# A Fourier layer's mix stage: the spectrum loaded block-diagonal from DRAM, and the row transform back on a half-sample grid

## The chip, the core and the metric

The kernel runs on one core of a Trainium2 chip. The metric is device time in microseconds from start to end of one execution. The core has a matrix engine (TensorE, PE in the profile, with its weight loads as PEld), three engines for elementwise work (VectorE or DVE, ScalarE or ACT, GpSimd or POOL) and SyncE (SP), whose queue issues most DMA transfers; POOL issues the others. Data lies in DRAM, in SBUF (128 lanes, called partitions) and in PSUM, where matmuls write. Everything is in float32, and each float32 matmul appears in the trace as two passes, each with its own weight load.

## What is computed

The input `x` is 16 images of 16 channels of 256 x 256. Two layers run one after the other, each as `x + layer(group_norm(x))`. The change lies in the first, a Laplace neural operator; the second (small convolutions, an involution and a channel gate) is not touched. The first layer, cut to what matters here:

```python
alpha = fft2(x)                                     # per image and channel
A  = 1 / (omega1[:, None, None, None] - pole1)      # [row frequency o, in i, out k, p]
Bm = 1 / (omega2[:, None, None, None] - pole2)      # [column frequency x, i, k, q]
S  = einsum('ikpq,oikp,xikq->oxik', residue, A, Bm)
output_residue1 = einsum('biox,oxik->bkox', alpha, S)
x1 = ifft2(output_residue1).real
# x2: a second term from the poles, summed elsewhere
return x1 + x2 / Nx / Ny
```

For every pair of frequencies `(o, x)` a 16 x 16 complex matrix `S` mixes the channels of all images; then the spectrum is transformed back. Since the images are real, about half of the row frequencies `o` suffice.

## The kernel before

**The stages.** `layer0_forward` transforms the images and writes the spectrum to DRAM as `al[33, 2, 64, 16, 256]`: 33 groups of four row frequencies, real and imaginary part `v`, 64 = (frequency `j` or `f` of the group, channel), image `b`, column frequency `x`. `layer0_mix`, the stage that changes, forms `S`, mixes and transforms back along the columns into `hd` in DRAM. `layer0_back` transforms back along the rows and adds `x2`. `layer1` is the second layer. The stages run one after the other.

**The forward transform of columns** (`wxn`, L1436 to 1443) uses a table of cosines and sines; its even and odd column frequencies stand in the two halves of a row, so the 256 values of `al` have a parity in front and the frequency behind.

**The mix stage, group by group (L752 to 779).** The order on PE, ACT, DVE and POOL is the order in which the code is written; SP and the DMA transfers follow by their dependences. For one group `g`:

- `mix` (L669) computes, for each of the 256 column frequencies `i`, one matmul (line 679) with the weights `s[:, i]`, 128 lanes by 32 columns, and as moving operand `alb[:, i]`, 64 columns. `alb` is block-diagonal: its 128 lanes are the parts, channels and four row frequencies, its 64 columns are four blocks of 16 images, and a lane is nonzero only in the block of its own frequency. Four column frequencies run side by side in four column strips of PE. ACT copies each 16 x 64 block of results from PSUM to `y` (L686).
- `residues` (L648) makes `s` for the next group: eight calls, each with matmuls (line 656) of `lt` by the table `tt`, and a copy out of PSUM by DVE or ACT (L665, L667). `s` exists once, so it begins when the mix has ended. `lt` comes from `poles` (L634), three DVE products (L640) from the plane-wise reciprocals `av`, which `load_poles` fetches two groups ahead on SP.
- `turn` (L688) transposes `y` for one row frequency `f` on PE, and DVE and ACT copy the result to `yt`.
- `columns` (L704) transforms back along the columns: for two halves `q`, even and odd column frequencies `e`, two `c` and two parts `v` a matmul (line 714) with `yt` as weights (64 lanes by 128 columns) and 256 columns of the table `ix`. Even and odd sums stand in one PSUM tile `ph`. ACT copies the odd half to SBUF (L723); DVE forms `even + odd` and `even - odd`, the two halves of the row (L726, L727), in the tile `h`, of which there are five buffers. POOL issues two stores to `hd` for each `q` (L734). For `f` of 3 the columns are spread into the mix of the next group (`between`).
- `load_spectrum(g, q)` (L602) fetches a quarter of the group's spectrum (four images) into one of four buffers `alc`, in four transfers of 32 lanes by 4 KB each, on SP (L607). `expand` (L613) multiplies a buffer by a lane mask `m4` into one of the four column blocks of `alb` and so writes data and zeros alike: 16 expansions for a group, six on ACT (L617) and ten on DVE (L619), dealt out by `spreads` (L622) between the turns and columns of the group before. `alb` exists once, 64 KB of every lane, its innermost order being frequency block and image.

Of the kernel before, what the change touches and what calls it, by code (L numbers as in the profile page):

```python
# [10 lines left out]
F32 = mybir.dt.float32  # L11
# [554 lines left out]
def layer0_mix(ctx, tc, d, al, hd, tabs):  # L566
# [32 lines left out]
    pst = ctx.enter_context(tc.tile_pool(name="pst", bufs=2, space=PSUM))  # L599
    psh = ctx.enter_context(tc.tile_pool(name="psh", bufs=2, space=PSUM))  # L600

    def load_spectrum(g, q):  # L602

        t = gp.tile([P, 4, 2, P], F32, tag="alc", name="alc", bufs=4)
        src = al[g].rearrange("v (j h c) b x -> h (v j) c (b x)", h=4, c=4)
        for h in range(4):
            nc.sync.dma_start(  # L607
                out=t[32 * h : 32 * h + 32].rearrange("p b e x -> p (b e x)"),
                in_=src[h, :, :, 4 * q * N : 4 * q * N + 4 * N],
            )  # L610
        return t

    def expand(t, q, j, eng):  # L613

        dst = alb.rearrange("p (x e) j b -> p b e x j", e=2)[:, 4 * q : 4 * q + 4, :, :, j]
        if eng is nc.scalar:
            eng.activation(dst, t, AF.Copy, scale=m4[:, j : j + 1])  # L617
        else:
            eng.tensor_scalar(dst, t, m4[:, j : j + 1], None, ALU.mult)  # L619


    spreads = (  # L622
# [4 lines left out]
    )  # L627

    def spread(spectrum, f):
        for eng, parts in zip((nc.scalar, nc.vector), spreads[f]):  # L630
            for q, j in parts:
                expand(spectrum[q], q, j, eng)

    def poles(av):  # L634


        lt = lp.tile([P, 32, 3, 4, 4], F32, tag="lt", name="lt")
        shape = [P, 32, 4, 4]
        for plane in range(3):
            nc.vector.tensor_tensor(  # L640
                lt[:, :, plane],
                av[:, :, :, plane].unsqueeze(3).to_broadcast(shape),
                m16.unsqueeze(1).unsqueeze(2).to_broadcast(shape),
                ALU.mult,
            )
        return lt.rearrange("p (k g) l f c -> p k g l f c", g=4)

    def residues(lt, s, k0):  # L648

        kk = k0 // 2  # L650
        ps = psg.tile([P, 2, 2, N], F32, tag="pg", name="ps")
        for v in range(2):
            for g in range(4):
                for odd in range(2):
                    lanes = slice(64 * odd, 64 * odd + 64)
                    nc.tensor.matmul(
                        ps[32 * g : 32 * g + 32, odd, v],
                        lhsT=lt[lanes, kk, g, 1 - v : 3 - v].rearrange("p l f c -> p (l f c)"),
                        rhs=tt[lanes, kk, g],
                        start=True,  # L660
                        stop=True,
                    )
        dst, src = s[:, :, :, k0 : k0 + 2], ps.rearrange("p k v x -> p x v k")
        if kk % 2:
            nc.vector.tensor_copy(dst, src)  # L665
        else:
            nc.scalar.copy(dst, src)  # L667

    def mix(s, y, between):  # L669


        for x0 in range(0, 64, 16):
            if x0 >= 32:
                next(between, None)
            ps = psg.tile([P, 16, 64], F32, tag="pg", name="pg")
            for x in range(16):
                for q in range(4):
                    i = 4 * (x0 + x) + q
                    nc.tensor.matmul(  # L679
                        ps[32 * q : 32 * q + 32, x],  # L680
                        lhsT=s[:, i].rearrange("p v k -> p (v k)"),
                        rhs=alb[:, i].rearrange("p j b -> p (j b)"),
                        start=True,
                        stop=True,
                    )
            nc.scalar.copy(y[:, :, x0 : x0 + 16], ps.rearrange("p x j -> p j x"))  # L686
# [16 lines left out]

    def columns(g, f, yt):  # L704

        ph = [psh.tile([P, 2, N], F32, tag="ph", name="ph") for q in range(2)]
        for e in range(2):
            if e:
                yield
            for n, (c, v) in enumerate(((0, 0), (0, 1), (1, 0), (1, 1))):  # L710
                i = 2 * (2 * c + e) + v
                for q in range(2):
                    lanes = slice(64 * q, 64 * q + 64)
                    nc.tensor.matmul(  # L714
                        ph[q][:, e],
                        lhsT=yt[lanes, i].rearrange("p t k -> p (t k)"),
                        rhs=ix[lanes, i],
                        start=n == 0,
                        stop=n == 3,
                    )  # L720
        for q in range(2):
            odd = hp.tile([P, 2, P], F32, tag="odd", name="odd", bufs=2)
            nc.scalar.copy(odd, ph[q][:, 1].rearrange("p (v x) -> p v x", v=2))  # L723
            o = hp.tile([P, 2, 2, P], F32, tag="h", name="h", bufs=5)
            even = ph[q][:, 0].rearrange("p (v x) -> p v x", v=2)
            nc.vector.tensor_tensor(o[:, :, 0], even, odd, ALU.add)  # L726
            nc.vector.tensor_tensor(o[:, :, 1], even, odd, ALU.subtract)  # L727
            o = o.rearrange("p v h x -> p v (h x)")
            fy = 4 * g + f
            for v in range(2):  # L730

                if fy % P or v == 0:
                    part = fy // P if fy % P == 0 else v
                    nc.gpsimd.dma_start(  # L734
                        out=hd[fy % 2, part, fy % P // 2, q:nb:2].rearrange("b k x -> b (k x)"),
                        in_=o[:, v],
                    )

    E = mybir.EngineType
    with tc.manual_schedule(engines={E.PE, E.Activation, E.DVE, E.Pool}):  # L740
# [6 lines left out]
        for q in range(4):  # L747
            spread(spectrum, q)
        for q in range(4):
            spectrum[q] = load_spectrum(1, q)  # L750
        between = iter(())
        for g in range(NF):  # L752
            more = g + 1 < NF
            y = gp.tile([P, 64, 64], F32, tag="y", name="y")
            if more:
                lt = poles(av)
            mix(s, y, between)
            if more:
                s = gp.tile([P, N, 2, C], F32, tag="s", name="s")
                residues(lt, s, 0)  # L760
            for f in range(4 if more else 1):
                if more and f == 3:
                    spread(spectrum, f)
                    for k0 in (12, 14):
                        residues(lt, s, k0)
                yt = turn(y, f)
                if more:
                    for k0 in range(2 if f == 0 else 4 * f, 4 * f + 4, 2) if f < 3 else ():
                        residues(lt, s, k0)
                    if f < 3:  # L770
                        spread(spectrum, f)
                    if g + 2 < NF:
                        if f == 0:
                            av = load_poles(g + 2)
                        spectrum[f] = load_spectrum(g + 2, f)
# [646 lines left out]
def fourier_tables():  # L1422
# [5 lines left out]
    def parities(a):  # L1428
# [4 lines left out]
    fy[:, 0, 1, 0] = cos[:P, P]  # L1433
    wx = np.stack([cos, -sin, sin], axis=1)

    wxn = np.stack(  # L1436
        [
            np.stack([np.concatenate([cos[:P, e::2], -sin[:P, e::2]], 1),
                      np.concatenate([sin[:P, e::2], cos[:P, e::2]], 1)], axis=1)
            for e in (0, 1)  # L1440
        ],
        axis=1,
    )

    ix = np.stack([np.concatenate(a, 1) for a in ((cos[:, :P], sin[:, :P]), (-sin[:, :P], cos[:, :P]))], 1)
    ix = np.tile(ix.reshape(64, 8, N), (2, 1, 1))

    iy = np.stack([cos[:P], -sin[:P]], axis=1) / (N * N)
    iy[0, 0] *= 0.5
# [6 lines left out]
    for t in tt:  # L1456
# [21 lines left out]
        "m4": np.tile(np.repeat(np.eye(4), 4, axis=0), (8, 1)),  # L1478
# [76 lines left out]
```

## Time and profile before

| what | value |
|---|---|
| median of 3 runs | 6919.16 us (6918.71 to 6933.95) |
| the profiled execution | 6939.37 us, span 6937.6 us, mean granted clock 0.967 |
| forward, 0 to 1381 us | PE busy 1244.8 us, DVE 1094.7, DMA share 0.42 |
| mix stage, 1381 to 2781 us | PE busy 1204.2 us, DVE 869.6, ACT 802.8, POOL 439.6, DMA share 0.36 |
| back, 2781 to 3430 us | PE busy 602.3 us, DMA share 0.93 |
| second layer, 3430 to 6937 us | PE busy 3324.0 us, DVE 2928.1, DMA share 0.85 |

The rows on the stages are the busy times of the engines in stretches of the trace. In the groups of instructions of the mix stage, `L714 PE MATMUL ph` takes 507.9 us in all, the mix's `L679 PE MATMUL pg` 311.6, the residues' `L656` 272.4, the transposes' `L695` 141.6; the expansions take 424.1 us of DVE (330 of 1415 ns) and 387.5 us of ACT (198 of 2059 ns). A group line reads: line, engine, operation, written tile, read tiles, sizes, count, then busy time, mean length in ns, and idle time before it with what ended it. "issue" means that nothing in the profile explains the wait. "DMA share" is the mean busy share of the 16 DMA engines. The rows on code transfers are called "instruction".

### The profile page before, as it was taken

The numbers are of one execution on the slowest core, as the hardware profiler recorded it, in microseconds if no ns is written. First come the engines' busy times: TensorE is split into PE (matmuls) and PEld (weight loads), VectorE is DVE, ScalarE is ACT, GpSimd is POOL, SyncE is SP. The second block draws the span as 40 slices with busy tenths as digits, with TensorE's granted clock in tenths as the row PEclk, the third lists the DMA queues.
The fourth block names the chain that finished last, engine by engine and source line by source line (L and its number), as shares of the span: only waits on it lengthen the run. The fifth ranks groups of instructions, "written<-read, shape, count | busy, mean of one in ns | idle before, by whom it ended". The sixth has DMA issues, their size and how long they took to land.

```text
span 6937.6 us, 153382 instructions
## 1 busy us (share of the span) xinstructions
PE 6375.2 (92%) x59944; PEld 3583.2 (52%) x59944; DVE 5451.1 (79%) x10057; ACT 3703.9 (53%) x5732; POOL 3635.8 (52%) x4614
## 2 busy tenths in 40 slices
PE   7899989978888888899789999999999999999996
PEld 5777777766766677677533333333333333333331
DVE  8888987356666666788788888888888888888885
ACT  1223333355655555222376666666666666666671
POOL 2334544523333333666665666666766566665563
PEclk9999999989999999999899999999999999999998
DMA  3444434433333333999877898888988889988886
GB/s 95 124 123 122 122 112 119 113 123 104 111 108 111 110 104 93 318 327 326 281 209 231 272 285 261 264 274 277 286 267 261 272 267 285 287 262 262 272 272 211
DMA packets 715941, 1443.97 MB, mean 208 GB/s; under 512 B 101338, under 2 KB 523542, under 8 KB 672950
## 3 DMA queue, kind: packets, MB, share of 16 engines
q1 hardware_dynamic: 567030, 959.77, 45.0%
q0 software_dynamic: 148192, 474.40, 21.8%
q8 instruction: 478, 7.83, 0.5%
q14 instruction: 241, 1.97, 0.1%
HBM read 877.12 MB, written 556.47 MB: 207 GB/s over the span
## 4 chain that ended last, share of the span: by engine, by line
PE 65%; DVE 20%; DMA 5%; issue 5%; ACT 4%; POOL 1%; SPq 0%; DVEq 0%; ACTq 0%; POOLq 0%
PE c2ps L1201 17%; PE c L1053 14%; PE pd L1121 13%; PE pg L679 4%; PE ph L714 3%; DVE alb L619 3%; ACT wide L1101 3%; PE px L313 2%; PE pu L207 2%; PE py L876 2%; PE pr L1080 2%; PE pv L214 2%; DVE u L224 2%; PE py L877 2%; DVE st L174 1%
## 5 line engine op out<-in xcount | busy, mean ns | idle before, releaser
L1101 ACT ACTIVATE wide<-c,b 32x512 f32<-32x512 f32 x2176 | 1479.6, 680 | 311.6 <-PE c L1053 263.5
L1132 DVE TENSOR_TENSOR top<-pd,t 32x512 f32<-32x512 f32 x2176 | 1504.0, 691 | 52.6
L1053 PE MATMUL c<-z,w 102*128 102x512 f32 x2048 | 999.7, 620 | 110.7 <-ACT wide L1101 89.3
L1113 POOL COPY wide<-wide 32x1031 f32<-32x1031 f32 (+1 forms) x576 | 579.7, 1006 | 881.5 <-ACT wide L1101 854.4
L1129 DVE TENSOR_TENSOR t<-pd,r 64x512 f32<-64x512 f32 x1088 | 744.1, 684 | 345.3 <-PE pd L1121 298.2
L1121 PE MATMUL pd<-wide,dw 128*128 128x512 f32 x2048 | 988.6, 604 | 12.0 <-DVE top L1132 11.0
L734 POOL DMA_DIRECT2D hd<-h x512 | 434.8, 856 | 955.0 <-DVE h L727 937.0
L1053 PEld LDWEIGHTS c<-z,w 102*128 102x128 f32 x2048 | 371.7, 192 | 697.5 <-issue 462.5
L1201 PE MATMUL c2ps<-rows,c 128*32 128x512 f32 x6144 | 721.6, 602 | 5.6 <-DVE odd L1228 5.6
L1121 PEld LDWEIGHTS pd<-wide,dw 128*128 128x128 f32 x2048 | 380.9, 192 | 572.2 <-issue 418.5
L1114 POOL COPY wide<-wide 32x1031 f32<-32x1031 f32 (+1 forms) x576 | 576.0, 1000 | 33.5
L1072 ACT ACTIVATE bot<-c,b 128x512 f32<-128x512 f32 x544 | 344.4, 684 | 462.6 <-issue 381.4
L714 PE MATMUL ph<-ix,yt 64*128 64x256 f32 x4128 | 507.9, 394 | 17.6 <-DVE yt L701 14.7
L313 PE MATMUL px<-wxn,u 128*64 128x256 f32 x4224 | 481.5, 379 | 2.4 <-ACT o L320 2.4
L207 PE MATMUL pu<-fy,eo 128*128 128x128 f32 x2048 | 436.2, 297 | 42.0 <-DVE u L224 35.2
L714 PEld LDWEIGHTS ph<-ix,yt 64*128 64x128 f32 x4128 | 419.6, 192 | 89.9 <-ACT s L667 29.6
L679 PE MATMUL pg<-alb,s 128*32 128x64 f32 x16896 | 311.6, 237 | 154.1 <-issue 71.8
L1201 PEld LDWEIGHTS c2ps<-rows,c 128*32 128x32 f32 x6144 | 174.8, 108 | 513.5 <-issue 404.5
L889 POOL TENSOR_TENSOR x<-x,o 128x512 f32<-128x512 f32 x256 | 324.4, 1267 | 217.3 <-DVE o L888 197.5
L619 DVE TENSOR_SCALAR alb<-alc,m 128x1024 f32<-128x1024 f32 x330 | 424.1, 1415 | 0.0
L214 PE MATMUL pv<-at,eo 128*128 128x128 f32 x2048 | 423.0, 291 | 0.0
L726 DVE TENSOR_TENSOR h<-ph,odd 128x256 f32<-128x256 f32 x258 | 113.4, 440 | 389.4 <-ACT odd L723 389.4
(221 smaller groups left out, 11460.2 us busy)
## 6 DMA issues: line engine op xcount, KB each, us to landing
rows<-cf SPq DMA_DIRECT2D x128, 2176.0 KB
z<-zn SPq DMA_DIRECT2D x768, 257.8 KB
cf<-top POOLq DMA_DIRECT2D x512, 240.0 KB, 6.9
cf<-bot POOLq DMA_DIRECT2D x96, 840.0 KB, 10.8
alc<-al SPq DMA_DIRECT2D x528, 128.0 KB
zn<-zb SPq DMA_DIRECT2D x128, 516.0 KB
o<-zn SPq DMA_DIRECT2D x128, 516.0 KB
z<-in_x SPq DMA_DIRECT2D x64, 1024.0 KB
```

Source lines behind the costliest of these rows:

```text
L313: nc.tensor.matmul(ps[64 * k : 64 * k + 64, :, h], lhsT=u[:, h, part, g0 + j + k].rearrange("p f c -> p (f c)"), rhs=wxn[:, h, part], star ...
L619: eng.tensor_scalar(dst, t, m4[:, j : j + 1], None, ALU.mult)
L679: nc.tensor.matmul(ps[32 * q : 32 * q + 32, x], lhsT=s[:, i].rearrange("p v k -> p (v k)"), rhs=alb[:, i].rearrange("p j b -> p (j b)"), s ...
L714: nc.tensor.matmul(ph[q][:, e], lhsT=yt[lanes, i].rearrange("p t k -> p (t k)"), rhs=ix[lanes, i], start=n == 0, stop=n == 3,)
L1053: nc.tensor.matmul(ps[:, a], lhsT=w, rhs=z[:k, c : c + 2, 0:N], start=True, stop=True)
L1101: nc.scalar.activation(self.feat[64 - 32 * q : 96 - 32 * q, f, self.groups[g], :H], ps[q][32 * f : 32 * f + 32], AF.Mish, bias=b1[0][32 * ...
L1113: nc.gpsimd.tensor_copy(flat[0:32, f, 1:m], flat[64:96, f, 0 : m - 1])
L1114: nc.gpsimd.tensor_copy(flat[96:128, f, 0 : m - 1], flat[32:64, f, 1:m])
L1121: nc.tensor.matmul(ps, lhsT=dwt if self.tail else dw, rhs=self.feat[:, f, cs, :H], start=True, stop=True,)
L1129: nc.vector.tensor_tensor(t[64:128], ps[:64], self.r[:, cs], ALU.mult)
L1132: nc.vector.tensor_tensor(self.top[32 * f : 32 * f + 32, cs, q], ps[lanes], t[lanes], ALU.add)
L1201: nc.tensor.matmul(ps[32 * j : 32 * j + 32], lhsT=w[:, blk], rhs=src[:, 4 * j + blk : 4 * j + blk + 4, x : x + H], start=(i, blk) == (0, 0 ...
```

## The change

**The spectrum.** `alb` gets the order lane, frequency block `f`, image `b`, column frequency `x`, and is cleared once at the start, half by DVE and half by POOL. `load_spectrum(g)` writes each piece of a group's spectrum from DRAM into its own diagonal block: 16 transfers for a group, for each `f` and each quarter `h` of the channels, onto 8 lanes (two parts by four channels), 16 KB for each lane. The blocks off the diagonal stay zero. The buffers `alc`, the mask `m4`, `expand`, `spreads` and `spread` go. The transfers for group `g + 1` stand after `mix` of group `g`, since the one `alb` is read until then. In `mix` the moving operand is `spectra[:, :, x]`: its 64 columns lie 1 KB apart.

**The transform back.** The forward table `wxn` takes its frequencies at half-sample positions (`cosh`, `sinh` of `(2k + 1)k'`), and `ix` correspondingly. On that grid the four quarters of a row are sums and differences of two symmetric and two antisymmetric sums of 64 columns, so `ix` has 128 columns for 256. `columns` makes as many matmuls as before, each with 128 columns, into blocks of `ph` chosen by the part `v`. ACT copies the antisymmetric half; DVE forms their sum and, mirrored, their difference in a tile `w`; from the two parities of `w` DVE forms the outer quarters and POOL the inner ones, mirrored.

**The poles.** `lt` is laid out by part, so that `poles` is two products of 1024 elements for each lane where it was three of 512, and a weight load of `residues` reads consecutive elements.

```diff
-    ix = load(nc, cp, d["ix"], [P, 8, N], "ix")
-    alb = cp.tile([P, N, 4, nb], F32, name="alb")
-    m4 = load(nc, cp, d["m4"], [P, 4], "m4")
+    ix = load(nc, cp, d["ix"], [P, 8, P], "ix")
+    alb = cp.tile([P, 4, nb, N], F32, name="alb")
+    nc.vector.memset(alb[:, :2], 0.0)
+    nc.gpsimd.memset(alb[:, 2:], 0.0)
+    spectra = alb.rearrange("p f b x -> p (f b) x")
...
-    def load_spectrum(g, q):
-        t = gp.tile([P, 4, 2, P], F32, tag="alc", name="alc", bufs=4)
-        src = al[g].rearrange("v (j h c) b x -> h (v j) c (b x)", h=4, c=4)
-        for h in range(4):
-            nc.sync.dma_start(
-                out=t[32 * h : 32 * h + 32].rearrange("p b e x -> p (b e x)"),
-                in_=src[h, :, :, 4 * q * N : 4 * q * N + 4 * N],
-            )
-        return t
+    def load_spectrum(g):
+        src = al[g].rearrange("v (f h c) b x -> h f v c (b x)", f=4, h=4)
+        for f in range(4):
+            for h in range(4):
+                lanes = slice(32 * h + 8 * f, 32 * h + 8 * f + 8)
+                nc.sync.dma_start(
+                    out=alb[lanes, f].rearrange("p b x -> p (b x)"), in_=src[h, f]
+                )
...
-        lt = lp.tile([P, 32, 3, 4, 4], F32, tag="lt", name="lt")
-        shape = [P, 32, 4, 4]
-        for plane in range(3):
+        lt = lp.tile([P, 2, 32, 4, 2, 4], F32, tag="lt", name="lt")
+        shape = [P, 128, 2, 4]
+        for v in range(2):
             nc.vector.tensor_tensor(
-                lt[:, :, plane],
-                av[:, :, :, plane].unsqueeze(3).to_broadcast(shape),
-                m16.unsqueeze(1).unsqueeze(2).to_broadcast(shape),
+                lt[:, v].rearrange("p k f l c -> p (k f) l c"),
+                av.rearrange("p k f l -> p (k f) l")[:, :, 1 - v : 3 - v].unsqueeze(3).to_broadcast(shape),
+                m16.unsqueeze(1).unsqueeze(1).to_broadcast(shape),
                 ALU.mult,
             )
...
-                        rhs=alb[:, i].rearrange("p j b -> p (j b)"),
+                        rhs=spectra[:, :, N // 2 * (i % 2) + i // 2],
...
-            for n, (c, v) in enumerate(((0, 0), (0, 1), (1, 0), (1, 1))):
-                i = 2 * (2 * c + e) + v
-                for q in range(2):
-                    lanes = slice(64 * q, 64 * q + 64)
-                    nc.tensor.matmul(
-                        ph[q][:, e],
-                        lhsT=yt[lanes, i].rearrange("p t k -> p (t k)"),
-                        rhs=ix[lanes, i],
-                        start=n == 0,
-                        stop=n == 3,
-                    )
+            for v in range(2):
+                blocks = slice(0, 4, 3) if v == 0 else slice(1, 3)
+                for c in range(2):
+                    i = 2 * (2 * c + e) + v
+                    for q in range(2):
+                        lanes = slice(64 * q, 64 * q + 64)
+                        nc.tensor.matmul(
+                            ph[q][:, e, blocks],
+                            lhsT=yt[lanes, i].rearrange("p t k -> p (t k)"),
+                            rhs=ix[lanes, i].rearrange("p (b x) -> p b x", b=2),
+                            start=c == 0,
+                            stop=c == 1,
+                        )
...
-            odd = hp.tile([P, 2, P], F32, tag="odd", name="odd", bufs=2)
-            nc.scalar.copy(odd, ph[q][:, 1].rearrange("p (v x) -> p v x", v=2))
-            o = hp.tile([P, 2, 2, P], F32, tag="h", name="h", bufs=5)
-            even = ph[q][:, 0].rearrange("p (v x) -> p v x", v=2)
-            nc.vector.tensor_tensor(o[:, :, 0], even, odd, ALU.add)
-            nc.vector.tensor_tensor(o[:, :, 1], even, odd, ALU.subtract)
+            anti = hp.tile([P, 2, 2, 64], F32, tag="anti", name="anti", bufs=2)
+            nc.scalar.copy(anti, ph[q][:, :, 2:])
+            w = hp.tile([P, 2, 2, 2, 64], F32, tag="w", name="w")
+            sym = ph[q][:, :, :2]
+            nc.vector.tensor_tensor(w[:, 0], sym, anti, ALU.add)
+            nc.vector.tensor_tensor(w[:, 1, :, :, ::-1], sym, anti, ALU.subtract)
+            o = hp.tile([P, 2, 4, 64], F32, tag="h", name="h", bufs=5)
+            parts = o.rearrange("p v s x -> p s v x")
+            nc.vector.tensor_tensor(parts[:, 0::3], w[:, :, 0], w[:, :, 1], ALU.add)
+            nc.gpsimd.tensor_tensor(parts[:, 2:0:-1], w[:, :, 0], w[:, :, 1], ALU.subtract)
...
-        spectrum = [load_spectrum(0, q) for q in range(4)]
+        load_spectrum(0)
...
             mix(s, y, between)
             if more:
+                load_spectrum(g + 1)
                 s = gp.tile([P, N, 2, C], F32, tag="s", name="s")
                 residues(lt, s, 0)
```

More of the change, by code (lines that the diff above doesn't have):

```diff
@@ L704, in columns @@
     def columns(g, f, yt):
-        ph = [psh.tile([P, 2, N], F32, tag="ph", name="ph") for q in range(2)]
+        ph = [psh.tile([P, 2, 4, 64], F32, tag="ph", name="ph") for q in range(2)]
         for e in range(2):
@@ L769, in layer0_mix @@
                         residues(lt, s, k0)
[L770 to L775, printed above, removed]
+                    if f == 0 and g + 2 < NF:
+                        av = load_poles(g + 2)
                 between = columns(g, f, yt)
@@ L1434, in fourier_tables @@
     wx = np.stack([cos, -sin, sin], axis=1)
+    half = np.outer(2 * k + 1, k) % (2 * N) * (TWO_PI / (2 * N))
+    cosh, sinh = np.cos(half), np.sin(half)
     wxn = np.stack(
         [
-            np.stack([np.concatenate([cos[:P, e::2], -sin[:P, e::2]], 1),
-                      np.concatenate([sin[:P, e::2], cos[:P, e::2]], 1)], axis=1)
+            np.stack([np.concatenate([cosh[:P, e::2], -sinh[:P, e::2]], 1),
+                      np.concatenate([sinh[:P, e::2], cosh[:P, e::2]], 1)], axis=1)
             for e in (0, 1)
```

29 lines of the change are left out of this document (6 added, 23 removed), and 4 rows, old and new, of the table spreads.

## The prediction

> **What bounds the kernel now.** I read the page first, then the mix alone: its busy time by engine, its waits, the timeline of one group, and the DMA rows of four stretches. In the timeline (start us, length us, engine, line, operation, count, idle before) one group, from the mix at 2003.88 to the next at 2045.67, is:
>
> ```profile
> 2003.88 3.45 PE L679 MATMUL pg<-alb,s 128*32 128x64 f32 x160 [2.08 <-DVE s L665]
> 2009.21 2.79 PE L679 MATMUL pg<-alb,s 128*32 128x64 f32 x96 [1.88 <-issue]
> ...
> 2011.93 2.00 PE L714 MATMUL ph<-ix,yt 64*128 64x256 f32 x16
> ...
> 2017.70 1.99 PE L679 MATMUL pg<-alb,s 128*32 128x64 f32 x128
> ...
> 2023.08 3.72 PE L714 MATMUL ph<-ix,yt 64*128 64x256 f32 x32
> ...
> 2028.28 19.01 SPq L607 DMA_DIRECT2D alc<-al  x16
> ...
> 2045.67 3.32 PE L679 MATMUL pg<-alb,s 128*32 128x64 f32 x125 [2.16 <-DVE s L665]
> ```
>
> The first mix starts at 1412.55 and the 33rd at 2754.86, so a group lasts 1342.3/32 = 41.95 us. PE is busy 87% of it and sets the pace. Two parts: the mix itself, 2003.88 to 2019.7 (in the next group 2045.67 to 2061.8, so 16.2 us), though its passes need only 4 x 1.99 us and the two half columns 2 x 2.0; and 25.7 us of residues, turns and columns, closed by a wait of 2.16 us for DVE's copy of `s`, which stands behind the expansions. The 4 us missing in the mix are "issue": code comes in pieces of 16 KB, and the DMA rows of 2003 to 2020 show
>
> ```profile
> q8 instruction: 4, 0.07, 1.6%
> ```
>
> four pieces for 576 passes, one per 3.6 us or so. The spectrum costs nothing today: four `alc` buffers are refilled behind the expansions, long before they are wanted.
>
> **The part that decides: the load.** The expansions and the masks go. The spectrum is written straight into `alb`, of which there is one copy (64 KB of each lane), and every matmul of the mix reads all lanes of it. So group g+1's 16 transfers start when the last `pg` pass of group g has ended, and mix g+1 starts when the last of them has landed. The period becomes mix + load, and all other work lies inside the load. How fast is the load? It moves the same 2.097 MB, but a transfer is now `[v=2, c=4, 4096]` from DRAM onto 8 lanes, where it was `[(v j)=8, c=4, 1024]` onto 32. How many of the 16 DMA engines take part is seen in two stretches in which only one kind of hardware transfer runs. First `alc`, with a backlog behind it (windows, last columns clock, DMA share, GB/s; then its DMA rows):
>
> ```profile
> 1389.00:1395.00 6.00, 4.16 (x96) 2.15 (x96) 1.73 (x2) 2.11 (x2) 0.00 (x0) 0.58 1.00 413
> 1396.00:1403.00 7.00, 2.84 (x96) 1.49 (x80) 4.76 (x5) 4.30 (x4) 0.00 (x0) 0.85 0.51 200
> ```
>
> ```profile
> DMA packets 427, 1.40 MB, mean 200 GB/s; under 512 B 85, under 2 KB 85, under 8 KB 427
> ```
>
> 85 of 427 packets are tiny and 342 hold 4 KB: 8 tiny ones to each transfer's 32. The share is 0.51 although transfers are queued (issue began at 1389): the same 8 engines each time. Its outer source dimension is 8, its destination has 32 lanes. Next the 24 loads of ten rows onto ten lanes at L1044 (3560 to 3580):
>
> ```profile
> q1 hardware_dynamic: 486, 1.00, 17.9%
> ...
> z<-zn SPq DMA_DIRECT2D x24, 40.2 KB
> ```
>
> 486/24 = 20: 10 rows and 10 tiny packets, where 16 engines would give 26 and a count of 624. So a transfer runs on as many engines as its smaller outer dimension counts. In the new load that is v = 2. I take 2 engines, always the same ones, as with `alc`; the other end, 8 engines by its lanes, is rival A.
>
> [...]
>
> Each of two engines then moves 1.049 MB. Per busy engine the windows give 413/16 = 25.8 GB/s, where larger packets run, and 200/(0.51 x 16) = 24.5 for 4 KB ones; with the `hd` stores in between, 1500 to 2700 gives q1 64.77 MB in 16.8% of 16 x 1200 us, or 20.1. The packets will be 16 KB, so I take 25.8: 40.6 us (ends 38, from 437 GB/s in the fullest slices of that stretch, and 52). The `hd` stores use all 16 engines,
>
> ```profile
> q0 software_dynamic: 36242, 59.53, 17.5%
> ```
>
> which is 0.175 x 41.95 = 7.3 us of each engine per group by packet time, 5.1 by bytes; three of four columns fall into the load: 4 us (0 to 5.5). Issue to first use: the chain of waits has 2.94 us from an `alc` issue's end to the expansion, of which 16 KB per engine are 0.67; with the 0.65 of one issue, 3.0 us (2.5 to 3.5); the other 15 issues (273 to 650 ns each) are hidden by the stream. Load: 40.6 + 4 + 3 = 47.6 us.
>
> On SP only `load_poles(g+2)` stands behind the waiting loads. It reaches the same two engines after them, so DVE's `poles` of the next group start when the mix does; the `lt` they write is wanted after the mix, 16 us later.
>
> **The mix.** Same passes, same code bytes, 16.2 us. Shorter column halves inside it give code no more speed, so I count no gain; the pause before it lets perhaps 2 us of code wait ready, and its low clock takes something back (14 to 18). The moving operand now has its 64 elements 1 KB apart. No row shows a strided one on PE. DVE's strided write at L224 takes 588 ns against 440 for the same size packed: from 1.0 to 1.34, and 1.34 x 1.99 = 2.7 us per 128 passes still lies under the 3.6 of code. I take nothing. [...]
>
> **What is hidden.** Per group: ACT loses 6 x 2.06 = 12.4 us, DVE 10 x 1.415 = 14.2. DVE gains 8 more sums of 128x256 between SBUF tiles (0.42, L546): 3.4; `poles` in two instructions of 1024 (1.24, L1191) for three of 512 (0.69): +0.4. POOL gains 8 subtractions (753 ns, L265), 6.0, ahead of the `hd` issues it already makes (16 x 0.86 = 13.8). PE: columns of 128 for 256, so 32 passes take between 1.86 us (half) and 3.35 (the weight loads' busy time) instead of 3.72. After the mix PE then has 25.7 - 2.2 - 3 x (0.4 to 1.9), or 18 to 22 us, inside 47.6. Were the cover gone, this work would be the path again, and the late `hd` stores (0.75 us of POOL each) would wait for one of five `h` buffers. The two clears of 8192 elements (3548 ns for 4128 at L1011, so 7 us) are paid once, under the first load.
>
> **The sum.** Period 16.2 + 47.6 = 63.8 us, 21.85 more, x 32 = 699. At the start the engines are full until 1395 (`tt` and `ix`; half an `ix` is 1.3 us), then 40.6 + about 2 until the first mix at 1436.5 instead of 1412.55: 24. Together +723. The profiled execution is 6939.4 us (span 6937.6 and 1.8 around it): 7662; the median shown is 20 lower, so 7642. I say 7640.
>
> **Rivals.** A: the 8 lanes decide, 8 engines. 2.097 MB at 200 GB/s is 10.5 us, with 3.0 and some `hd` under 18, within PE's 18 to 22 us. Period 34 to 38.6, 3.4 to 8 less, x 32: 6690 to 6830, say 6760, faster. For it: destination lanes are the outermost thing written; against it: `alc` had 32 lanes and used 8. It decides from 7 engines up, where the load (2.1 MB/(7 x 25.8) = 11.6, and 3 + 4) comes under PE's work. B: v and c are dealt out so that 4 engines work: 20.3 + 7 + 16.2 = 43.5, x 32 and the start: about 6975. Nothing in the rows shows such a deal. C: 8 engines, but the strided operand takes the place of the code. From 5 us per 128 passes (2.5 times the 1.99) it eats A's gain; at 4 times, 8 us, the mix is 34 us, the period 54, the time 7305. Against it: PE takes an element only about every 0.9 ns today (256 columns, 232 ns a pair).
>
> **How the numbers follow.** Two engines 0.85; A 0.09; B 0.03; C 0.03. Inside the forecast the ends are 14 + 2.5 + 38 + 0 = 54.5 (7345) and 18 + 3.5 + 42.8 + 5.5 = 69.8 (7840), or 71 with 20.1 GB/s (7880). All at one end at once is unlikely, so 7390 to 7870 holds most of the 0.85. About 0.3% can be told from no change: faster 0.10 (A and a little of B), same 0.02, slower 0.88.
>
> **What would show it.** In the mix's windows the DMA share during the load is about 0.13 for the loads alone, near 50 GB/s; before each mix PE waits some 25 us for a DMA onto `alb`; the clock sags there. DVE, ACT and POOL are idle over half of it. The `ph` passes and their length tell of the halved columns, the `pg` rows of the stride. It is wrong if the share during the load is near 0.5 and PE waits for no DMA.

## The result and the profile after

The changed kernel takes 8103.8 us (median of four runs, 8098.6 to 8114.0), the kernel before 6920.4 (median of four): a ratio of 1.1707 (95% interval 1.1687 to 1.1727). Slower, as forecast, but by 1180 us and not by 720: 8104 lies above the range of 7390 to 7870.

From the page of the changed kernel (the profile's summary of one execution): the span, the granted clock and the DMA share in 40 slices, three groups, and the DMA issues of the load.

```profile
span 8112.3 us, 152964 instructions
...
PEclk9999999878878788787899899999999999999998
DMA  3444444111111111111599878888888888888886
...
L659 PE MATMUL pg<-alb,s 128*32 128x64 f32 x16896 | 902.9, 405 | 957.0 <-DMA alb<-al 604.1
...
L708 DVE TENSOR_TENSOR w<-ph,anti 128x256 f32<-128x256 f32 x258 | 182.8, 709 | 1642.2 <-ACT anti L705 1642.2
...
L713 POOL TENSOR_TENSOR h<-w 128x256 f32<-128x256 f32 x258 | 238.4, 924 | 1730.2 <-DVE w L709 1727.9
...
alb<-al SPq DMA_DIRECT2D x528, 128.0 KB
```

In the twelve slices of the mix stage (the eighth to the nineteenth) the 16 DMA engines are busy a tenth of the time, and PE waits for a transfer onto `alb` before its `pg` passes: the load decides, as forecast. (604.1 of the 957.0 us are put down to that transfer; another 352.9 to the pole load that follows it on the same queue.) But the passes themselves have grown too. They are as many as before and as large, and their busy time went from 311.6 us (237 ns each) to 902.9 (405). Ahead of DVE's additions and POOL's subtractions these engines idle over 1600 us each.

One group in the timeline of the changed kernel (start us, length us, engine, line, operation, count, idle before):

```profile
2001.27 14.68 SPq L610 DMA_DIRECT2D alb<-al  x6
...
2038.20 13.99 PE L659 MATMUL pg<-alb,s 128*32 128x64 f32 x256 [28.45 <-DMA alb<-al]
...
2052.11 1.16 PE L696 MATMUL ph<-ix,yt 64*128 64x128 f32 x16
...
2053.21 7.57 PE L659 MATMUL pg<-alb,s 128*32 128x64 f32 x128
...
2061.80 7.65 PE L659 MATMUL pg<-alb,s 128*32 128x64 f32 x128
2061.95 7.34 ACT L705 COPY anti<-ph 128x256 f32<-128x256 f32 x2
2065.68 3.72 DVE L708 TENSOR_TENSOR w<-ph,anti 128x256 f32<-128x256 f32 x1 [48.08 <-ACT anti L705]
...
2069.48 14.38 SPq L610 DMA_DIRECT2D alb<-al  x12
...
2072.60 2.06 PE L696 MATMUL ph<-ix,yt 64*128 64x128 f32 x32
```

PE waits 28.45 us for the load, then needs 31 us for the mix; 128 `pg` passes, 1.99 us before, take 7.6. Two `anti` copies of ACT, which stand beside such passes, take 7.34 us, and 0.65 elsewhere. The half-width columns come out as forecast: 32 `ph` passes in 2.06 us (bounds 1.86 and 3.35).

The windows of the changed kernel for the load, the first half of that mix and its third quarter (busy us and count of PE, weight loads, DVE, ACT, POOL; then granted clock, DMA share, GB/s):

```profile
2020.00:2038.00 18.00, 0.00 (x0) 0.00 (x0) 0.00 (x0) 0.00 (x0) 0.00 (x0) 0.50 0.15 59
2038.00:2052.00 14.00, 13.80 (x256) 13.61 (x256) 0.00 (x0) 1.01 (x1) 0.00 (x0) 0.92 0.01 2
...
2053.00:2060.00 7.00, 7.00 (x127) 6.87 (x127) 0.00 (x0) 0.28 (x1) 0.00 (x0) 1.00 0.01 2
```

The DMA rows of the first window have for SP's queue

```profile
q1 hardware_dynamic: 88, 0.82, 10.8%
```

With the `hd` stores the DMA share is 0.15 and the rate 59 GB/s; SP's queue alone has 0.11 and, with 0.82 MB in 18 us, 46 GB/s (0.13 and 50 were forecast for the loads alone). A share of 0.108 is 1.7 of the 16 engines, so the two that were forecast. A 16 KB packet of a load took 614 ns (median of the stage), 26.7 GB/s; 64 of them on each of two engines are 39.3 us. The third line excludes the clock as the cause of slow passes: at full clock, with next to nothing else running, 127 of them fill 7 us.

From the first mix to the 33rd the period is 77.62 us (41.95 before). The stretch between mixes is 48.25, the mix 29.37 (means of 32 groups; before, 26.08 and 15.87). That makes 32 x 35.67 = 1141; the first mix starts 13 later than before, and what follows the 33rd mix's start is 20 longer, 14 of them this last mix itself. Together 1174, the difference of the two spans.

### The profile page after: what moved, and what is told of

It is laid out like the page before. It is cut to its first block, busy times and chain, and to the rows that moved or that the text cites. A ratio compares the mean times of both kernels' runs of the same rounds, so it can differ in the third digit from the quotient of the medians.

```text
span 8112.3 us, 152964 instructions
## 1 busy us (share of the span) xinstructions
PE 6722.9 (83%) x59944; PEld 3972.3 (49%) x59944; DVE 5289.3 (65%) x9953; ACT 3454.7 (43%) x5534; POOL 3742.8 (46%) x4873
## 5 line engine op out<-in xcount | busy, mean ns | idle before, releaser
L659 PE MATMUL pg<-alb,s 128*32 128x64 f32 x16896 | 902.9, 405 | 957.0 <-DMA alb<-al 604.1
L659 PEld LDWEIGHTS pg<-alb,s 128*32 128x32 f32 x16896 | 859.7, 153 | 978.1 <-issue 964.1
L708 DVE TENSOR_TENSOR w<-ph,anti 128x256 f32<-128x256 f32 x258 | 182.8, 709 | 1642.2 <-ACT anti L705 1642.2
L713 POOL TENSOR_TENSOR h<-w 128x256 f32<-128x256 f32 x258 | 238.4, 924 | 1730.2 <-DVE w L709 1727.9
L666 ACT COPY y<-pg 128x1024 f32<-128x1024 f32 x132 | 134.3, 1017 | 1661.4 <-PE pg L659 1661.4
L720 POOL DMA_DIRECT2D hd<-h x512 | 308.1, 605 | 287.7 <-DMA hd<-h 154.6
```

The lines of the kernel that those rows point to most:

```text
L659: nc.tensor.matmul(ps[32 * q : 32 * q + 32, x], lhsT=s[:, i].rearrange("p v k -> p (v k)"), rhs=spectra[:, :, N // 2 * (i % 2) + i // 2], ...
```

## The experiments

Two costs are to be told apart: the load between mixes and the operand's pitch. The rivals for the second were the pause itself (PE cold, or code late after it) and writes of the load that disturb the reads. Stretch and mix are measured in each trace as above, as means over 32 groups.

**The operand alone.** The pass takes 64 neighbouring numbers of the tile; all else stays:

```
-    rhs=spectra[:, :, N // 2 * (i % 2) + i // 2],
+    rhs=flat[:, 4096 * (i % 4) + 64 * (i // 4) : ... + 64],
```

> The changed kernel, but each matmul of the mix reads 64 neighbouring elements of `alb` (another 64 for each of the 256, spread over all four blocks), so it mixes other numbers and the output is not the reference's; the loads and their waits are as they were. Theory O (operand): 64 elements 1 KB apart feed PE several times slower than 64 neighbours. Then the mix falls from 29.3 us a group back to 14 to 16.5, the stretch between two mixes stays at 48.3, the period is some 64 us and the time 8104 - 33 x 13.5 = 7660 (7600 to 7720), which is also what the prediction's sum came to. Rival P (pause): the mix is long because PE has stood still for 28 us before it, at a low clock and with its code not fetched; then the mix stays near 29 us and the time at 8100.

Measured: 7575.3 us, ratio 1.0955 (1.0935 to 1.0975): the operand theory in its kind, 25 us below its range. The period is 61.31, and a mix ends 14.5 us after the last packet of its load, where the changed kernel needs 30.2. In this kernel a pass needs the lanes of one `f` only, so six passes of a mix go ahead while the load is under way, and the others start when it is over:

```profile
2045.98 6.48 PE L659 MATMUL pg<-alb,s 128*32 128x64 f32 x250 [10.74 <-DMA alb<-al]
```

PE has stood still for 25 us but for those six, the granted clock is 0.52 (window from 2046 to 2052), and 250 passes take 6.48 us where 256 took 13.99. So the pause is not it. Also seen in one view of both kernels, the instructions of a line (count, then ns of the shortest, the median and the longest). Of the changed kernel:

```profile
L705 ACT COPY anti<-ph x258: 372/378/5534, 1454.2 to 3944.6; 128x256 f32<-128x256 f32 x129
```

and of this one:

```profile
L705 ACT COPY anti<-ph x258: 372/374/380, 1454.3 to 3411.8; 128x256 f32<-128x256 f32 x129
```

The longest copy falls from 5534 ns to 380: PE's strided reads, not the copy's own form, had held ACT up. (It is not the load either: in the run without loads below, with the strided operand, the longest copy is 4636 ns.)

**Which pitch costs what.** One kernel gives each of eleven groups in turn another way through the tile (pitches in numbers of 4 bytes; the passes mix other numbers):

```
+    kind = (256, 1, 2, 4, 8, 16, 64, 257, "pairs", "fours", "same")[g % 11]
-    rhs=spectra[:, :, N // 2 * (i % 2) + i // 2],
+    rhs=moving(g, i),
```

> The changed kernel, with the pattern of the mix's moving operand changed from group to group (eleven patterns, three groups each): pitch 256 elements as it is, 1, 2, 4, 8, 16, 64, 257, then 32 pairs and 16 fours of neighbours 1 KB apart, and last pitch 256 with all four column strips reading the same column. It mixes other numbers; read from it is the length of the mix of each group. Theory L (lines of 16 bytes, 4 elements): pitch 1 as before (some 16 us), pitch 2 in between, pitch 4 and all above as slow as 256 (28 to 31 us), pairs as pitch 2, fours as pitch 1, and the same column no different. Theory B (banks, hit by the power of two): 257 is as fast as 1, and 64 or 256 slower than 4 or 8; pairs and fours help in proportion only. Theory S (the four strips get in each other's way): the same column is faster than 256.

The timeline of PE, one block of 128 passes each; in this order a pitch of 2, 4, 16, 64 and 257, then 256 with the same column in all strips, then 256 as in the change:

```profile
1566.05 2.38 PE L679 MATMUL pg<-alb,s 128*32 128x64 f32 x128
...
1628.69 3.98 PE L679 MATMUL pg<-alb,s 128*32 128x64 f32 x128
...
1757.74 3.96 PE L679 MATMUL pg<-alb,s 128*32 128x64 f32 x128
...
1828.80 7.77 PE L679 MATMUL pg<-alb,s 128*32 128x64 f32 x128
...
1901.81 3.97 PE L679 MATMUL pg<-alb,s 128*32 128x64 f32 x128
...
2096.75 7.77 PE L679 MATMUL pg<-alb,s 128*32 128x64 f32 x128
...
2175.28 7.08 PE L679 MATMUL pg<-alb,s 128*32 128x64 f32 x128
```

Two steps are to be seen (the whole kernel took 7777 us in its one run). At a pitch of 4, 8, 16 and 257 numbers (16 bytes and more) a block takes 4.0 us. At 64 and 256 the blocks shown take 7.1 to 7.8, nearly twice that again; over all groups they vary more, from 5.6 to 7.7 us in the changed kernel, 6.84 in the mean (902.9 us for 132 blocks). Runs of two or four neighbours within a long pitch keep PE busy 2.6 to 2.8 and 2.2 to 2.3 us in the last two blocks of a mix, the packed operand 2.0 to 2.3. None of the theories holds as written: L had a pitch of 4 as slow as 256, B had 257 as fast as 1. And that the four strips' different columns were the cost (S) is excluded: one column for all is no faster (7.77 us and 7.08). The first step lies between two numbers from each 16 bytes, 2.38 us, and one, 3.98. What makes it, and what makes 64 and 256 slower than 16 and 257, these runs do not show.

**257 in place of 256.** A column's run in `alb` gets one unused number behind it, which cuts the loads into pieces of 1 KB:

```
-    alb = cp.tile([P, 4, nb, N], F32, name="alb")
+    alb = cp.tile([P, 4, nb, N + 1], F32, name="alb")
```

> The changed kernel with one unused element behind every 256 of `alb`, so that the mix's 64 elements lie 1028 bytes apart and not 1024; the loads go on as before, in pieces of 1 KB. Computes the reference. From the sweep: pitch 257 takes 3.7 us for 128 passes where pitch 256 takes 7.4 and neighbours 2.2. Theory B+L (a doubling for a new 16-byte line at each element, a second one for the power of two): the mix falls from 29.3 to 4 x 3.7 + 2.3 = 17 us. The load grows with its packets, 1024 of 1 KB on each of two engines at 46 ns, 47 us for 39, so the stretch between is 56 for 48; period 73 for 77.6, time 8104 - 32 x 4.6 - 12 = 7945 (7850 to 8000). Rival (the sweep's gain came from what else was odd there, such as the strips' columns): the mix stays at 29 and the time goes to 8360.

Measured: 7934.7 us, ratio 1.1474 (1.1451 to 1.1496), as expected. (The 3.7 us that the expectation takes from the sweep is 4.0 in its trace, so the mix comes out at 17.8 and not at 17.) The mix falls to 17.8 us in all groups but the first, which has no columns in it (15.6), and the stretch rises to 54.3: of the 11.6 us that the better pitch gains, the smaller pieces give back 6.0. (A 1 KB packet on SP's queue takes 46 ns, the median in the trace of before, so 16 of them 736 ns; one of 16 KB takes 614 in the changed kernel.)

**No loads.** The 32 loads after the first are left out, with the operand as in the change and then packed:

```
             if more:
-                load_spectrum(g + 1)
```

> The changed kernel with the spectrum loaded once, before the first group; the other 32 loads are left out, so all groups mix with the first group's spectrum and the output is not the reference's. The load theory (the stretch between mixes is load alone, and the rest of PE's work would take 18 to 22 us there): mix 29.3, stretch 18 to 22, period 47.3 to 51.3 instead of 77.6, so 7130 to 7260 us, say 7190. Rival, that the load's writes into SBUF also slow the strided mix: they end before it begins, so the mix should not change; if it falls below 25 us, part of the mix's 29.3 belongs to the load and not to the operand. Rival, that the columns and the residues have grown too (as where the change's transform was put into the kernel before, with 28.9 us between mixes): period about 58, 7480.

> The same with the operand of a pass as 64 neighbouring numbers of the tile: other numbers of the spectrum are mixed and 32 loads are left out, the output is not the reference's. If load and stride are all that the change lost by, mix 13 to 16.2, stretch 18 to 22, period 31 to 38.2 instead of 77.6 and 41.95 before: 6610 to 6840, say 6720, faster than before. If the transform's part takes as long as it did alone in the kernel before (28.9 between mixes), the period is about 43 and the time about 7000, slower than before even then.

Measured: 7240.1 us, ratio 1.0457 (1.0423 to 1.0491), and 6729.4, ratio 0.9719 (0.9687 to 0.9751). The stretches are 20.7 and 21.1 us, inside the 18 to 22 that the prediction gave PE's remaining work; the mixes 29.5 and, after the first, 13.8. Both times lie in their ranges, and the mix has its 29 us without any load beside it. The four kernels make a square:

| | loads | no loads |
|---|---|---|
| strided | 8104 | 7240 |
| packed | 7575 | 6729 |

The stride costs 529 us with loads and 511 without, the load 864 and 846: they add up, and nothing of size lies between them. The timeline of the kernel without both, one mix:

```profile
2022.14 2.76 PE L659 MATMUL pg<-alb,s 128*32 128x64 f32 x180 [1.23 <-DVE s L645]
2026.28 1.31 PE L659 MATMUL pg<-alb,s 128*32 128x64 f32 x76 [1.38 <-issue]
```

There the wait for a transfer is gone and the unexplained wait ("issue") is back, as in the kernel before; that it is a wait for code is the prediction's reading, which no run here tests.

**More engines for the load.** `al` is laid out so that a transfer's source is eight whole rows; its lanes stay the same:

```
-    src = al[g].rearrange("v (f h c) b x -> h f v c (b x)", f=4, h=4)
+    src = al[g].rearrange("(f h c) v b x -> h f (c v) (b x)", f=4, h=4)
```

> The changed kernel with the spectrum stored as [33, 64, 2, 16, 256], so that a load's source is 8 rows of 16 KB one behind the other, onto the same 8 lanes (parts and channels change places within them, and `lt` with them). Computes the reference. Theory E (engines): the old load ran on 2 engines because its source had an outer dimension of 2; now 8 work, the load takes 10.5 + 3 + some hd, below PE's work after the mix; the stretch between two mixes falls from 48.3 to 18 to 22 us and the time to 8104 - 32 x 28 = 7200 (7100 to 7350). DMA share during the load near 0.5. Rival D (destination): 8 lanes take no more than two engines' worth, or 16 KB packets are slow by themselves; then the stretch stays over 40 us and the time near 8100.

Measured: 7767.3 us, ratio 1.1236 (1.1215 to 1.1257); the stretch is 38.2 us, not 20, and neither theory's numbers came. A window of the load in this kernel with the DMA row of SP's queue, then waits over the whole stage:

```profile
2012.00:2020.00 8.00, 6.50 (x88) 4.71 (x88) 2.87 (x7) 1.76 (x4) 2.71 (x4) 0.55 0.51 76
```

```profile
q1 hardware_dynamic: 60, 0.48, 38.9%
```

```profile
POOL hd L720 <- DMA hd<-h: 512.2, 136, 8.2
DVE h L712 <- DMA hd<-h: 492.7, 88, 12.7
...
PE pg L659 <- DVE s L645: 283.8, 30, 16.6
```

SP's queue alone now has a share of 0.39, six engines' worth, where it had 0.11. Of its 60 packets 29 are of 16 KB and 31 are tiny, so about eight tiny ones to a transfer's eight rows: counted as the prediction counted `alc`, eight engines. So far more than two take part, and the reading that the source's outer dimension held them to two was right here. But the packets are slower: a 16 KB packet takes 1851 ns (median of the stage) where two engines needed 614. From its first packet to its last the load takes 34.4 us, or 61 GB/s, for 46.0 us and 46 GB/s in the changed kernel (means of 32 groups). And it is not what PE waits for last: it is through 2.9 us before the mix begins, and PE waits 30 times, once a group, for DVE's copy of `s`. DVE waits for a free buffer `h`, whose stores take 18.2 us to land (median; 17.3 in the changed kernel, 4.2 before). Whether the eight lanes or the new order of the rows in DRAM slow the packets, this run does not show; the next ones bear on it.

**The loads on POOL's queue.** They leave SP, first alone and then with the pitch of 257:

```
-    nc.sync.dma_start(
+    nc.gpsimd.dma_start(
```

> [...] Computes the reference. Theory E2 (the same two engines every time is what makes the load slow, and the destination lanes of one transfer are what made eight engines crowd in the last attempt): if POOL's queue deals its transfers out to other engines each time, the stretch between mixes falls from 48.3 to what PE does after the mix or POOL needs for its issues, 20 to 27 us, period 49 to 56, time 8104 - 32 x 25 = 7300 (7150 to 7450). [...]

> The changed kernel with both: pitch 257 and the loads on POOL's queue. Computes the reference. If both costs are what the runs say and they add, the mix is 17 us and the stretch after it 20 to 27, a period of 37 to 44 against 41.95 of the kernel before: 6780 to 7000. Rival: the costs do not add, because a shorter mix leaves the load and the code pieces to meet; then above 7100.

Measured: 7468.6 us, ratio 1.0800 (1.0769 to 1.0830), just past the upper end, with a stretch of 29.2 us; and 7283.1, ratio 1.0531 (1.0517 to 1.0546), a mix of 17.8 and a stretch of 34.4: missed by 280 or more. In the first the load itself takes 19.1 us from its first packet to its last, 110 GB/s, with packets of 1174 ns (median). That is eight packets at a time (128 x 1174 ns in 19.1 us), about as many as with eight rows (seven). A transfer lands 7.9 us after its issue (median), so several of the 16 are under way at once, to different lanes. This speaks for the lanes as the limit there; queue and row order differ too. But the load begins 6.2 us after the mix, as POOL comes to it, and the next mix 3.9 us after the load. The waits of the second (us in total, times, longest):

```profile
PE ph L696 <- DVE yt L681: 366.3, 64, 12.5
DVE w L708 <- POOL h L713: 349.7, 54, 11.7
...
POOL alb L610 <- DMA alb<-al: 199.7, 162, 3.0
```

Read from below: POOL's issues of loads wait for earlier loads; behind them stand POOL's subtractions, behind these DVE's additions, and PE waits for DVE. A load on POOL's queue costs POOL time that PE's columns need: an issue takes 549 ns of POOL in the first, 847 in the second (medians), 16 to a group. The pitch acts here as it did alone: two `anti` copies beside the mix take 0.65 us again.

**The transform alone.** Into the kernel before go only the half-sample tables and the new `columns`; load, expansion and operand stay as before. (For a short diff see `columns`, `ix` and `wxn` of the change.)

> The kernel before with the transform back alone changed: `wxn`, `ix` and `columns` from the change, the masks and expansions kept. Computes the reference. Theory V (DVE): after the mix DVE is busy 23 of 26 us, and gets 8 sums of 0.42 more, so the shorter columns (2.06 us for 3.72, three of them in this stretch) are not seen; 6900 to 6960, no change. Rival T (PE sets the stretch): 3 x 1.66 = 5 us less a group, x 32: 6760.

Measured: 6978.6 us, ratio 1.0097 (1.0082 to 1.0111): a loss of one per cent from the part that shortens PE's work, 19 us above the range of theory V. The mix gets shorter, 14.5 us, and the stretch longer, 28.9 for 26.1. The timeline of this kernel before a mix:

```profile
2006.23 1.25 DVE L665 COPY s<-ps 128x1024 f32<-128x1024 f32 x1
...
2007.63 3.92 PE L679 MATMUL pg<-alb,s 128*32 128x64 f32 x160 [5.50 <-DVE s L665]
```

The wait for DVE's copy of `s`, 2.08 and 2.16 us in the groups shown of before, is now 5.5 (over the stage 136.5 us in 32 waits for 68.7 before): the eight extra additions stand before it on DVE. They are free only where DVE no longer expands the spectrum. Next, three of DVE's ten expansions were given to POOL:

```
-        (((0, 0), (1, 0)), ((0, 1), (0, 2), (0, 3))),
+        (((0, 0), (1, 0)), ((0, 1), (0, 2)), ((0, 3),)),
```

> The kernel before with the transform back alone changed, and three of DVE's ten expansions of a group given to POOL. Computes the reference. Theory V (DVE sets the stretch after the mix, which grew from 26.1 to 28.9 us when the transform back alone was changed): DVE loses 3 x 1.4 = 4.2 us, the stretch falls to some 25 us, the period from 43.4 to 39.5, the time to 6978 - 32 x 3.9 = 6850 (6800 to 6900), faster than the kernel before. Rival: POOL, whose subtractions and stores of `h` come behind the expansions, becomes the one that is waited for; 6950 to 7050.

Measured: 7043.6 us, ratio 1.0188 (1.0174 to 1.0202), a miss and a further loss; the rival came true. The groups of this line for the mix stage (busy us, mean ns, idle before):

```profile
L619 POOL TENSOR_SCALAR alb<-alc,m 128x1024 f32<-128x1024 f32 x98 | 429.2, 4381 | 18.0 <-issue 13.9 <-DMA alc<-al 0.9
L619 DVE TENSOR_SCALAR alb<-alc,m 128x1024 f32<-128x1024 f32 x228 | 411.6, 1896 | 0.0
```

An expansion takes POOL 4381 ns, and DVE's own, 1415 before, take 1896 beside it. DVE has seven expansions a group for ten and is busy with them for about as long as before (411.6 us for 424.1), and PE now waits 178 us for POOL's expansions.

**Two versions meant to win.** Rows of 257 numbers in DRAM too, so that loads are whole rows and the pitch is 257; the 16 loads of a group shared by two queues, SP and POOL, then SP and ACT:

```
+    al = dram.tile([NF, 64, 2, nb, N + 1], F32, name="al")
...
+    alb = cp.tile([P, 4, nb, N + 1], F32, name="alb")
...
+        for h in range(4):
+            for f in range(4):
+                queue = nc.sync if f < 2 else nc.gpsimd
```

> A version meant to beat both kernels, with what the runs so far showed put together: the spectrum lies in DRAM with the 8 rows of a transfer together and 257 numbers to a column's run, so a load is still whole rows (16.4 KB packets) but the operand's numbers lie 1028 bytes apart; of the 16 loads of a group eight go out on SP's queue and eight on POOL's, taking turns through other lanes. The mix should be that of the run with both mends, 17.8 us, not 29.3. If the loads of the two queues go to different lanes at once and so run at twice the 54 GB/s or so that eight lanes took, the load is 2.097 MB at 108 GB/s = 19.4 us, with 3 of start and 0 to 4 of hd stores 22 to 27 between mixes: period 40 to 45 (41.95 before), 6900 to 7060 us, say 6980: about as before or a little slower. Rival: the eight lanes' limit stays whatever the queue, and the stretch is 38 as with 8 rows on SP: period 56, 7410. Rival: POOL's eight issues (0.55 us each and waits) delay its subtractions and so DVE and PE: stretch about 30, period 48, 7150.

> The last kernel with its eight POOL loads per group issued by ACT instead (eight by SP as there), so that POOL makes none. The mix stays at 17.8 us. With two queues the stretch between mixes was 29.0, with POOL's issues waiting 330 us for earlier transfers in all (10 a group) and DVE behind POOL. If POOL's issues were the cause, and the transfers of the two queues go to different lanes at the same time, the stretch falls to 22 to 27 and the period to 40 to 45 (41.95 before): 6900 to 7060 us, say 6990. Rival: all loads now use the same 8 engines, as with 8 rows on SP, and the hd stores and pieces of code stand behind them: stretch 30 to 38, period 48 to 56, 7150 to 7400.

Measured: 7115.4 us, ratio 1.0291 (1.0270 to 1.0313), with a mix of 17.8 and a stretch of 29.0; and 7405.4, ratio 1.0707 (1.0689 to 1.0725), with 17.8 and 38.2. Both missed. The load itself was through 25.2 and 26.0 us after the mix (24.1 and 24.8 us from first packet to last, 87 and 85 GB/s), faster than the 34.4 us of eight rows on one queue, which again speaks for the lanes; the rows in DRAM are 257 numbers long here, which was not tried by itself. (The 54 GB/s that the first expectation gives to eight lanes is near the 55 that 2.097 MB make over the whole stretch of 38.2 us with eight rows; from first packet to last it was 61.) But the next mix began 3.8 and 12.3 us after it. In the first the rival came true that POOL's issues are late, as the waits of that kernel show:

```profile
POOL alb L612 <- DMA hd<-h: 330.5, 93, 8.7
```

In the second the rival's numbers came, but not for its reason: the stores land in 3.0 us (median), and it is ACT that is held, by its own issues:

```profile
ACT s L649 <- DMA alb<-al: 539.9, 33, 24.3
PEld ph L698 <- ACT yt L681: 512.2, 33, 19.2
```

ACT copies `s` and `yt` for PE, and PE waits 15.5 us a group for it (512.2/33). So each of POOL's and ACT's queues had other work behind it, and on SP's alone the load was too slow. None of the versions with the new load comes under the kernel before; the nearest is 2.9% over it.

## Why the prediction was right in its sign and wrong in its size

Its sum gave a span of 7661 us (6937.6 and 723), the trace shows 8112: 451 are missing. By its terms:

- **The part that decides: the load.** Right. Forecast 47.6 us between mixes, measured 48.25; 32 x 0.65 = 21. That it came so near is partly luck: the packets of two engines need 39.3 us for 40.6, start and end 2.3 for 3, and what else these engines carry, the `hd` stores above all, the remaining 6.7 for 4.
- **The mix.** This is the step that failed. "I take nothing" for the strided operand, with 1.34 as its upper bound, gave 16.2 us; measured 29.37, 32 x 13.17 = 421 of the 451. The bound came from the nearest row, but that row was of another engine and of a write, and so bounded nothing for PE's read. The price of rival C, "at 4 times, 8 us", was near what came (6.84 in the mean, 3.4 times the 1.99, and up to 7.7). But the prediction joined it to eight engines only, where it is a rival; with two engines it is a term of the forecast. Its own numbers, 34 for the mix and 47.6 for the load, would have given a period of 81.6 and an upper end of some 8210, above the result. Nor is 13.17 the whole price of the stride: from the load's last packet to the mix's end it was 30.2 us, packed 14.5, so 15.7 a group.
- **What is hidden.** Right: without loads the stretch is 20.7 to 21.1 us, in the 18 to 22 named, and all of it lies inside the load.
- **The start and the end.** Forecast 24, measured 13 at the first mix (-11); 8.6 of that is that the stage began earlier in this profile (the first table `tt` is issued at 1369.5 and not at 1378.1; over all runs 1369.5 to 1386.8), which has nothing to do with the sum. At the end the last mix, which has no load behind it, is longer by the same stride, +20 with what follows, which the sum had not counted. 21 + 421 - 11 + 20 = 451.
- **Rival A** was priced wrongly, apart from its condition. It took 200 GB/s, seen at 32 lanes, for a transfer onto eight. In the run with eight rows the load moved 61 GB/s, and the stretch was 38.2 us and not under 18.

What the change would be worth without its two costs is shown by the run without loads and with a packed operand: a period of 35.8 for 41.95, 2.8% off the time. That kernel loads nothing after the first group, so this is the most that was to be had. What is shown: the stride costs 0.5 ms, the load behind the mix 0.85, independently. Not tried: a second copy of `alb`, by which the load could run under the mix.

## What to carry to other kernels

A layout that makes a transfer long and simple can make the operand of every pass slow: price the reader's pitch by itself, and if no row shows the operation on that engine, keep the range open to several times the packed cost in every case, not in one rival. Two or more numbers from each 16 bytes kept 128 passes near their packed time here, even in short runs (2.2 to 2.8 us, packed 2.0 to 2.3, one number 4.0); of the pitches tried, 64 and 256 numbers were the worst (5.6 to 7.9). A load that writes the only copy of a buffer was paid in full between its readers (46.0 us of a stretch of 48.25). More engines alone need not speed it up much: six engines' worth gave 61 GB/s where two gave 46, and where transfers went to different lanes at the same time it was 85 to 110 (queue and row order differed too). And an issuing engine that had to wait held up the work behind it: for ACT, 539.9 us before its copies of `s`.

## What the runs showed of the hardware that was not expected

- PE's read of a column at a pitch of 64 or 256 numbers took 1.4 to 2 times as long as at 4, 8, 16 or 257 (5.6 to 7.9 us and 4.0 per 128 passes of 64 columns).
- The granted clock did not change the time of the strided pass: at a pitch of 257 a block took 4.0 us at 0.50 (the first one from 2634.6 in the run with eleven patterns) as at 1.00. The pairs took 3.6 at 0.50 and 2.6 to 2.8 at 1.00.
- Such reads held up other engines. Beside reads at a pitch of 256 ACT's copy of 128x256 took up to 5534 ns for 378, DVE's addition of `w` up to 5253 for 423, and POOL's subtraction between two tiles in SBUF up to 2506 for 748 (times on POOL are rough). With the packed operand the longest are 380, 426 and 1292; at the pitch of 257 (loads on POOL) 381, 426 and 1732. With the stride and no loads they are 4636, 2825 and 13386, so it is not the loads' writes. What this cost the period was not measured by itself.
- With eight DMA engines on a transfer's eight lanes in place of two, a 16 KB packet took 1851 ns in place of 614 (the order of the rows in DRAM differs too).
- `hd` stores landed late beside a load of 16 KB packets on SP's queue, on two engines (17.3 us, median of the stage) as on eight (18.2). Beside the same load in pieces of 1 KB on two engines they took 5.4, before the change 4.2, without loads 2.9.
